# Layer 1's first norm ahead of the biases, and score matmuls with 64 keys, in a kernel of two layers on Trainium2

## The chip, the cores and the metric

The kernel runs on one core of one Trainium2 chip, as one launch. The metric is the time of a run on the device in microseconds (us). Times before are those of three runs; beside them stands one execution that the hardware profiler recorded.

## What is computed

The input x is an image of 64 by 64 places with 256 channels, all in float32. Two layers follow one another. The places are called tokens in layer 1 (4096 tokens of 256 channels).

```
# layer 0: group norm, then a linear attention over boxes of the image
q, k = sigmoid(Wq xn), sigmoid(Wk xn);  v = Wv xn / |v|        # 8 heads of 32 channels
for w in (1, 2, 4):                # box of 64/w by 64/w places around each place, edge padded
    out_w = q . boxsum(k v^T) / (q . boxsum(k) + 1e-6)
x = x + Wout concat(out_1, out_2, out_4) + bout
# layer 1: attention, then a mixture of experts
t = t + softmax(q k^T / 16) v W_out + b_out,   (q, k, v) = norm(t) w_qkv + b_qkv
t = t + sum over the best 2 of 8 experts:  weight * (gelu(xe W1 + b1) W2 + b2),  xe from norm(t)
```

In layer 0 the kernel doesn't form the box sums for every place alone: it multiplies queries with single keys, masks the scores by what lies in the box, and multiplies with v, for the parts of a box that whole-cell sums don't cover. So both layers have scores, keys times queries.

## The kernel before

The engines are called PE (matmuls), PEld (its weight loads), DVE (vector), ACT (scalar), POOL and SP. The image is cut into 8 chunks of 512 tokens, each of 4 tiles of 128 tokens; a tile is two cells of 64 tokens. The 8 heads are worked in two halves (g) of four heads; a head's 32 channels lie on 32 partitions, so four heads fill the 128 partitions. A scheduler that orders the instructions stands between this text and the engines: each engine has one queue, worked in order, and the order in it follows from the program's order and from what each instruction waits for. `tc.issue_after(ins)` puts what follows behind `ins` in its engine's queue, without a wait of its own.

**Layer 0.** `prepare` (L307) makes sigmoid(q), sigmoid(k) and v for one half: `by_channel` (L353) computes q and k and its activation at L365 is the sigmoid. `attend` (L584) makes scores, masks them and multiplies with v, for boxes of three reaches. A step holds one or more pieces (up to 512 queries together). For the edges in y (L612) the scores of a tile are made 64 keys at a time: a matmul loads 32 partitions by 64 columns of k as weights and streams the queries. For the edges in x (L681) they are made 128 keys at a time. `masked` (L548) multiplies with the masks: DVE from PSUM directly, or ACT copies (L557) and POOL multiplies (L561). The products with v are at L643 and L697. Divisions (L721, L728) and projections (L734, L738) of a strip are chores between later steps. A root of one number at L252 lets ACT load the table of the square root early in layer 0, where L158 needs it.

**The seam.** When layer 0's last projection has freed its memory, the weights and biases of layer 1 are requested (L792 to L816, on the queues of ACT and SP). Then come, in the text's order: the biases of q and k turned to columns (L818, L820), products of the router's weights with ones and with the output bias (L827), the output weights turned (L841, L842) and multiplied with the router's (L846, L853). Then the norm: `begin(c)` takes the statistics of a chunk's four tiles (L764, L765), adds 1e-5 (L769) and takes the root on ACT (L770). The loop over chunks calls `begin` one chunk ahead, takes the reciprocal (L773), norms each tile (L869), turns it (`to_channels`, L779, ACT's copy L780), makes q and k for the chunk (L885, DVE adds the bias at L889 and takes the peak at L890), then v and the router's raw logits (L896, L903, L904).

**The attention of layer 1.** Loops: 8 chunks of queries (qc), 2 halves (g), 32 tiles of keys (i); one i is called a turn here, one (qc, g) a block. A turn makes the scores of four heads for 128 keys and 512 queries (L994), two heads to each pair of PSUM banks, of which there are three. ACT takes the Exp of each pair (L1004) into one of four buffers `pe`. DVE adds `pe` to a running total (L1011, all tiles but the first and last of a block). The products with v of the turn before (L962) follow the scores on PE. Denominators are made at the end of a block, and during the blocks with g = 1 the projection of an earlier chunk is slipped in four times (L943).

A float32 matmul appears in the trace as two records, one for each pass, each with its own weight load. The experts (L1428 to L1465) and the output (L1505 to L1512) follow; the change doesn't touch them.

Of the kernel before, what the change touches and what calls it, by code (L numbers as in the profile page):

```python
# [22 lines left out]
F32 = mybir.dt.float32  # L23
# [7 lines left out]
P = 128  # L31
# [83 lines left out]
def tile_conv_attn_hybrid(ctx: ExitStack, tc: tile.TileContext, a: dict, out: bass.AP):  # L115
# [73 lines left out]
    with ExitStack() as phase:  # L189
# [23 lines left out]
        with (  # L213
# [34 lines left out]
                )  # L248


            root = small.tile([P, 1], F32, name="root")
            nc.scalar.sqrt(root, ident[:, :1])  # L252


# [43 lines left out]
        def residual(b):  # L298

            for i in range(NCH):  # L300
                last = nc.vector.transpose(
                    t[:, NB * i + b, :C].rearrange("p (j c) -> p j c", c=D),
                    rows[:, b].rearrange("p j (y i c) -> p j y i c", y=4, c=SW)[:, :, :, i, :],
                )
            return last.ins

        def prepare(g, prep, ps):  # L307

# [44 lines left out]
            def by_channel(n, i):  # L353

                pr = two_banks()
                for j in range(2):
                    for k in range(KC):
                        nc.tensor.matmul(
                            pr[:, j, :],
                            w3[:, k, n, :],  # L360
                            act[:, k, chunk(i + j)],
                            start=k == 0,
                            stop=k == KC - 1,
                        )
                nc.scalar.activation(qk[:, n, CH * i : CH * (i + 2)], pr.rearrange("p j n -> p (j n)"), AF.Sigmoid)  # L365


            st = prep.tile([P, NCH, SW, D], F32, tag="st", name="st", bufs=2)
# [215 lines left out]
        def attend(g, work, ps, qk, v, ssum, rec, woT):  # L584
# [6 lines left out]
            for w in (2, 1, 0):  # L591
# [71 lines left out]
                for ix in range(NCH):  # L663
# [12 lines left out]
                    for step in steps:  # L676
                        scs = [score() for _ in range(4)]
                        at, places = 0, []
                        for n, i, c0, c1, *mk in step:
                            for h in range(4):  # L680
                                nc.tensor.matmul(  # L681
                                    scs[h][:, at : at + n],
                                    kT[hs[h], tok(i)],
                                    qT[hs[h], CH * ix + CELL * c0 : CH * ix + CELL * c1],
                                    start=True,
                                    stop=True,
                                    skip_group_check=True,
                                )
                            places.append((at, n, i, c0, c1, *mk))
                            at += n  # L690
                        sms = masked(work, scs, at, joined((p[0], p[1], *p[-2:]) for p in places))
                        step_done()

                        def use(places=places, sms=sms, acc=acc, begun=begun, ix=ix, last=step is steps[-1], raw=raw, r=r):
                            for at, n, i, c0, c1, *_ in places:
                                for h in range(4):
                                    nc.tensor.matmul(  # L697
                                        acc[hs[h], CELL * c0 : CELL * c1],
                                        v[:, i, hs[h]],
                                        sms[h][:, at : at + n],  # L700
                                        start=not begun[0],
                                        stop=last and at == places[-1][0],
                                        skip_group_check=True,
                                    )
                                begun[0] = True
                            if last and r > 1:
                                nc.vector.tensor_add(raw[:, ix, :], acc, raw[:, ix, :])
                            elif last:
                                nc.scalar.copy(raw[:, ix, :], acc)

                        behind(lambda: None, use)
# [35 lines left out]
        for g in range(KC):  # L747
            with tc.tile_pool(name="c_prep", bufs=1) as prep, psum("c_ps1", 2) as ps:
                of = prepare(g, prep, ps)
            with tc.tile_pool(name="c_work", bufs=1) as work, psum("c_ps2", 1) as ps:  # L750
                attend(g, work, ps, *of)

# [22 lines left out]
    def to_channels(src, dst, ps):  # L775

        tp = ps.tile([P, CH], F32, tag="mm", name="ps_mm")
        for k in range(KC):
            nc.tensor.transpose(tp[:, tok(k)], src[:, tok(k)], ident)  # L779
        nc.scalar.copy(dst, tp[:, :C].rearrange("p (k n) -> p k n", k=KC))  # L780

    norm2 = Norm(keep, "ln2")


    with ExitStack() as phase:
# [15 lines left out]
        with (  # L801
# [12 lines left out]
            bo = row_on_all("L1_attn_b_out", C, win)  # L814
            bv = win.tile([P, C], F32, name="bv")
            nc.scalar.dma_start(bv, a["L1_attn_b_qkv"][2 * C :].partition_broadcast(P))  # L816
            tp = ps.tile([P, CH], F32, tag="mm", name="ps_mm")
            nc.tensor.transpose(tp[:, :6], rows6, ident[:6, :6])  # L818
            bqk = win.tile([P, 6], F32, name="bqk")
            nc.vector.tensor_copy(bqk, tp[:, :6])  # L820

            rp = ps.tile([P, CH], F32, tag="mm", name="ps_mm")
            for n, by in enumerate((lambda k: ones[:, :1], lambda k: bqk[:, 4 + k : 5 + k])):
                for k in range(KC):
                    nc.tensor.matmul(  # L827
                        rp[:, NE * n : NE * (n + 1)],
                        by(k).to_broadcast([P, P]),
                        wr[:, k, :],  # L830
                        start=k == 0,
                        stop=k == KC - 1,
                    )
            nc.vector.tensor_copy(wr_sum, rp[:, :NE])
            bo_wr = win.tile([P, NE], F32, name="bo_wr")
            nc.vector.tensor_copy(bo_wr, rp[:, NE : 2 * NE])
            woT = win.tile([P, KC, C], F32, name="woT")
            for j in range(KC):
                tp = ps.tile([P, CH], F32, tag="mm", name="ps_mm")
                for k in range(KC):  # L840
                    nc.tensor.transpose(tp[:, tok(k)], wo[:, k, tok(j)], ident)  # L841
                nc.vector.tensor_copy(woT[:, j, :], tp[:, :C])  # L842
            tp = ps.tile([P, CH], F32, tag="mm", name="ps_mm")
            for k in range(KC):
                for j in range(KC):
                    nc.tensor.matmul(  # L846
                        tp[:, NE * k : NE * (k + 1)],
                        woT[:, j, tok(k)],
                        wr[:, j, :],
                        start=j == 0,  # L850
                        stop=j == KC - 1,
                    )
            nc.vector.tensor_copy(wo[:, :, C:], tp[:, : KC * NE].rearrange("p (k e) -> p k e", e=NE))  # L853

            norm = Norm(small, "ln1")

# [4 lines left out]

            begin(0)
            for c in range(NCH):
                if c + 1 < NCH:
                    begin(c + 1)
                norm.end(NB * c, NB * (c + 1))
                for i in range(NB * c, NB * (c + 1)):
                    hn = work.tile([P, C], F32, name="hn")
                    nc.vector.tensor_scalar(  # L869
                        hn,  # L870
                        t[:, i, :C],
                        norm.mean[:, i : i + 1],
                        norm.rstd[:, i : i + 1],
                        op0=ALU.subtract,
                        op1=ALU.mult,
                    )
                    to_channels(hn, act[:, :, tok(i)], ps)

                    nc.gpsimd.tensor_add(t[:, i, :C], t[:, i, :C], bo)
                for s in range(2):  # L880
                    for g in range(KC):
                        m = KC * s + g
# [10 lines left out]
                for i in range(NB * c, NB * (c + 1)):  # L893
                    pv = ps.tile([P, CH], F32, tag="mm", name="ps_mm")
                    for k in range(KC):
                        nc.tensor.matmul(  # L896
                            pv[:, : C + NE],
                            act[:, k, tok(i)],
                            wqkv[:, k, 2 * C :],
                            start=k == 0,  # L900
                            stop=k == KC - 1,
                        )
                    nc.vector.tensor_add(v[:, i, :], pv[:, :C], bv)  # L903
                    nc.scalar.copy(t[:, i, C:], pv[:, C : C + NE])  # L904


            on_experts = lambda z: z.unsqueeze(2).to_broadcast([P, NT, NE])
# [41 lines left out]
        with tc.If(tame > 0) as branch:  # L949
            with (  # L950
# [33 lines left out]
                for qc in range(NCH):  # L984
                    for g in range(KC):
# [4 lines left out]
                        for i in range(NT):  # L990
                            sc = [two_banks() for _ in range(2)]
                            for hd in range(4):
                                hs = slice(D * hd, D * (hd + 1))
                                nc.tensor.matmul(  # L994
                                    sc[hd // 2][:, hd % 2, :],
                                    qk[hs, 1, g, tok(i)],
                                    qk[hs, 0, g, chunk(qc)],
                                    start=True,
                                    stop=True,
                                )  # L1000
                            pe = work.tile([P, 4, CH], F32, name="pe", bufs=4)
                            pairs = [slice(0, 2), slice(2, 4)]
                            for pair, s in zip(pairs, sc):
# [543 lines left out]
```

## Time and profile before

| what | us |
|---|---|
| median of three runs | 2913.63 |
| lowest and highest of them | 2911.81, 2914.61 |
| the profiled execution's own time | 2911.62 |
| its span in the profile | 2909.8 |
| PE busy in the span | 2769.2 |
| DVE busy | 2082.3 |
| ACT busy | 1529.6 |
| POOL busy | 712.4 |

The span runs from the first to the last instruction that the profile shows; the profiled execution's own time is 1.8 us longer than it. Times in views of the profile count from the start of the span. In a timeline a row is: start, length of the merged group, engine, line, operation, what it writes and reads, how many instructions, and in brackets the idle time before it and what ended that. Matmuls overlap in the array and their ends are modelled, so the starts of two groups tell more than a group's length. In a table by stage each engine's busy time stands with its number of instructions, then the granted clock of PE (1.00 is full), the share of the DMA engines and GB/s.

### The profile page before, as it was taken

What the parts mean: (1) busy time and instruction counts of PE and PEld (TensorE: products, weight loads), DVE (VectorE), ACT (ScalarE), POOL (GpSimd) and SP (SyncE); (2) the same over time, 40 slices, a digit from 0 to 9 for tenths busy, and PEclk for the clock granted to TensorE, in tenths of its full rate; (3) what the DMA queues carried; (4) which work ended last, traced back from release to release, by engine and by line L of the source; (5) the groups of instructions that cost most, each with busy time, mean ns of one, the idle gap of its engine ahead of it and who ended that gap; (6) DMA issues with size and microseconds to landing.
All of it is one profiled execution on the core that took longest, in us unless ns stands there. A gap on an engine that the chain in (4) does not pass through costs nothing. (4 is left out here: it accounts for less than half of the span.)

```text
span 2909.8 us, 62928 instructions
## 1 busy us (share of the span) xinstructions
PE 2769.2 (95%) x26286; PEld 1329.9 (46%) x26286; DVE 2082.3 (72%) x3009; ACT 1529.6 (53%) x2134; POOL 712.4 (24%) x808
## 2 busy tenths in 40 slices
PE   6899999989999988999999999999999969999996
PEld 5466442735644254222222222222222248888884
DVE  6776777577676886999999999999999941111113
ACT  3242323124233312888888888888888642222222
POOL 1085858109485711000000000000000012222220
PEclk9999999999999999999999999999999969999997
DMA  5000000000000000000000000000000056565665
GB/s 143 6 2 3 2 3 2 7 0 3 4 2 3 1 19 1 1 5 6 5 5 5 5 5 5 5 5 5 5 5 5 10 176 215 190 203 196 205 213 189
DMA packets 97546, 136.31 MB, mean 47 GB/s; under 512 B 18115, under 2 KB 79145, under 8 KB 97253
## 3 DMA queue, kind: packets, MB, share of 16 engines
q1 hardware_dynamic: 82360, 105.34, 11.2%
q0 software_dynamic: 6528, 17.83, 2.2%
q10 hardware_dynamic: 8364, 9.02, 0.9%
q8 instruction: 209, 3.42, 0.5%
q14 instruction: 85, 0.69, 0.1%
HBM read 114.57 MB, written 17.60 MB: 45 GB/s over the span
## 5 line engine op out<-in xcount | busy, mean ns | idle before, releaser
L1004 ACT ACTIVATE pe<-ps_two 128x1024 f32<-128x1024 f32 x1024 | 993.1, 1022 | 152.2 <-PE ps_two L994 146.9
L1011 DVE TENSOR_TENSOR total<-total,pe 128x1024 f32<-128x1024 f32 x928 | 1058.2, 1219 | 2.2 <-ACT pe L1004 2.2
L994 PE MATMUL ps_two<-qk 32*128 32x512 f32 x4096 | 630.6, 640 | 3.5 <-POOLq L949 1.8
L962 PE MATMUL ps_acc<-pe,v 128*32 128x512 f32 x4096 | 547.2, 605 | 0.1
L557 ACT COPY sm<-ps_sc 128x384 f32<-128x384 f32 (+4 forms) x486 | 232.5, 513 | 460.6 <-PE ps_sc L681 271.2
L561 POOL TENSOR_TENSOR sm<-sm,mask 128x192 f32<-128x192 f32 (+3 forms) x460 | 380.2, 860 | 232.7 <-ACT sm L557 232.5
L994 PEld LDWEIGHTS ps_two<-qk 32*128 32x128 f32 x4096 | 205.2, 183 | 419.5 <-PE ps_two L994 221.3
L561 DVE TENSOR_TENSOR sm<-ps_sc,mask 128x384 f32<-128x384 f32 (+3 forms) x708 | 324.1, 518 | 92.8 <-PE ps_sc L681 91.4
L1456 ACT ACTIVATE hid<-ps_hp,cols 128x256 f32<-128x256 f32 (+1 forms) x288 | 133.1, 462 | 360.4 <-PE ps_hp L1453 359.3
L1271 POOL MEMSET on<- 128x256 f32 x1 | 0.3, 311 | 1177.3 <-PE ps_den L962 1177.3
L962 PEld LDWEIGHTS ps_acc<-pe,v 128*32 128x32 f32 x4096 | 80.8, 108 | 390.3 <-issue 377.2
L681 PE MATMUL ps_sc<-qk 32*128 32x192 f32 (+3 forms) x2688 | 245.3, 446 | 5.7 <-DVE sm L561 2.9
L1453 PE MATMUL ps_hp<-xe,w 128*128 128x256 f32 (+1 forms) x1152 | 246.6, 370 | 0.0
L1462 PE MATMUL ps_yp<-w,hid 128*128 128x256 f32 x1088 | 240.8, 379 | 0.0
L1453 PEld LDWEIGHTS ps_hp<-xe,w 128*128 128x128 f32 x1152 | 201.1, 190 | 39.7 <-ACT hid L1456 5.6
L697 PE MATMUL ps_acc<-sm,v 128*32 128x192 f32 (+3 forms) x2688 | 216.6, 423 | 0.8 <-POOL sm L561 0.8
L1462 PEld LDWEIGHTS ps_yp<-w,hid 128*128 128x128 f32 x1088 | 204.2, 190 | 26.4
L1432 DVE TENSOR_SCALAR xe<-ps_tp,cols 128x256 f32<-128x256 f32 (+1 forms) x72 | 34.8, 525 | 239.3 <-PE ps_tp L1428 217.5
L561 POOL TENSOR_TENSOR sm<-sm,ycut 128x384 f32<-128x384 f32 (+4 forms) x150 | 150.8, 1024 | 140.9 <-ACT sm L557 140.6
L681 PEld LDWEIGHTS ps_sc<-qk 32*128 32x128 f32 x2688 | 126.3, 186 | 124.5 <-DVE sm L561 70.1
L561 DVE TENSOR_TENSOR sm<-ps_sc,ycut 128x512 f32<-128x512 f32 (+4 forms) x250 | 127.7, 562 | 65.2 <-PE ps_sc L612 63.2
L1464 DVE TENSOR_TENSOR y<-ps_yp,b 128x256 f32<-128x256 f32 x68 | 28.9, 425 | 195.1 <-PE ps_yp L1462 195.1
(239 smaller groups left out, 2244.3 us busy)
## 6 DMA issues: line engine op xcount, KB each, us to landing
w<-in_L_ffn_W SPq DMA_DIRECT2D x72, 1024.0 KB
b<-in_L_ffn_b SPq DMA_DIRECT2D x36, 128.0 KB
rows<-in_x SPq DMA_DIRECT2D x16, 256.0 KB
zrows<-act SPq DMA_DIRECT2D x4, 1024.0 KB
y<-yrows SPq DMA_DIRECT2D x8, 512.0 KB
y<-yrows ACTq DMA_DIRECT2D x8, 512.0 KB
rec<-recs SPq DMA_DIRECT2D x60, 64.0 KB
x<-in_x ACTq DMA_DIRECT2D x4, 512.0 KB
```

The source lines that it names most:

```text
L557: nc.scalar.copy(sm[:, :used], sc[:, :used])
L561: engine.tensor_mul(to, of, mk.unsqueeze(1).to_broadcast(list(to.shape)))
L681: nc.tensor.matmul(scs[h][:, at : at + n], kT[hs[h], tok(i)], qT[hs[h], CH * ix + CELL * c0 : CH * ix + CELL * c1], start=True, stop=True, ...
L697: nc.tensor.matmul(acc[hs[h], CELL * c0 : CELL * c1], v[:, i, hs[h]], sms[h][:, at : at + n], start=not begun[0], stop=last and at == plac ...
L962: nc.tensor.matmul(to[D * hd : D * (hd + 1), :], lhsT(hd), rhs[:, hd, :], start=start, stop=stop, skip_group_check=True,)
L994: nc.tensor.matmul(sc[hd // 2][:, hd % 2, :], qk[hs, 1, g, tok(i)], qk[hs, 0, g, chunk(qc)], start=True, stop=True,)
L1004: nc.scalar.activation(pe[:, pair, :], s, AF.Exp, scale=C**-0.5)
L1011: add = nc.vector.tensor_add(to, first[:, pair, :] if i == 1 else to, pe[:, pair, :])
L1432: nc.vector.tensor_scalar(xe[:, k, :n], tp[:, k, :n], cols[:, gain], cols[:, shift], op0=ALU.mult, op1=ALU.add,)
L1453: nc.tensor.matmul(hp[:, :n], w1[:, k, tok(m)], x_now[:, k, :n], start=k == 0, stop=k == KC - 1)
L1456: nc.scalar.activation(hid[:, m, :n], hp[:, :n], AF.Gelu, bias=cols[:, m : m + 1])
L1462: nc.tensor.matmul(yp, hid[:, m, tok(j)], w2[:, m, :], start=m == 0, stop=m == NH - 1)
```

## The change

Four things are changed.

- In `attend` the scores of a step with a single piece are made 64 keys at a time (two matmuls with half the weights each); other steps keep 128.
- In the attention of layer 1 all scores are made 64 keys at a time.
- The root of one number is taken a second time, behind the last sigmoid of the second half of layer 0.
- At the seam the text's order is changed: statistics, norm and turning of chunk 0 come first, with four buffers for normed tiles; the bias columns and the statistics of chunk 1 are put behind them, and the router's products behind chunk 0's v.

```
-            root = small.tile([P, 1], F32, name="root")
+            root = wts.tile([P, 1], F32, name="root")
             nc.scalar.sqrt(root, ident[:, :1])
...
+        sigmoid = [None]
...
-                nc.scalar.activation(qk[:, n, CH * i : CH * (i + 2)], pr.rearrange("p j n -> p (j n)"), AF.Sigmoid)
+                sigmoid[0] = nc.scalar.activation(qk[:, n, CH * i : CH * (i + 2)], pr.rearrange("p j n -> p (j n)"), AF.Sigmoid).ins
...
                         for n, i, c0, c1, *mk in step:
+                            rows = CELL if len(step) == 1 else P
                             for h in range(4):
-                                nc.tensor.matmul(
-                                    scs[h][:, at : at + n],
-                                    kT[hs[h], tok(i)],
-                                    qT[hs[h], CH * ix + CELL * c0 : CH * ix + CELL * c1],
...
+                                for u in range(0, P, rows):
+                                    nc.tensor.matmul(
+                                        scs[h][u : u + rows, at : at + n],
+                                        kT[hs[h], P * i + u : P * i + u + rows],
+                                        qT[hs[h], CH * ix + CELL * c0 : CH * ix + CELL * c1],
...
                 of = prepare(g, prep, ps)
+            if g == KC - 1:
+                with tc.issue_after(sigmoid[0]):
+                    nc.scalar.sqrt(root, ident[:, :1])
...
+            def biases():
+                tp = ps.tile([P, CH], F32, tag="mm", name="ps_mm")
+                nc.tensor.transpose(tp[:, :6], rows6, ident[:6, :6])
+                nc.vector.tensor_copy(bqk, tp[:, :6])
+
+            def router():
...
             begin(0)
             for c in range(NCH):
-                if c + 1 < NCH:
+                if 0 < c < NCH - 1:
                     begin(c + 1)
                 norm.end(NB * c, NB * (c + 1))
                 for i in range(NB * c, NB * (c + 1)):
-                    hn = work.tile([P, C], F32, name="hn")
-                    nc.vector.tensor_scalar(
+                    hn = work.tile([P, C], F32, name="hn", bufs=4)
+                    last = nc.vector.tensor_scalar(
...
-                    to_channels(hn, act[:, :, tok(i)], ps)
+                    turned = to_channels(hn, act[:, :, tok(i)], ps)
...
+                if c == 0:
+                    with tc.issue_after(last.ins), tc.issue_after(turned.ins):
+                        biases()
+                        begin(1)
...
+                if c == 0:
+                    with tc.issue_after(biased.ins), tc.issue_after(product.ins):
+                        router()
...
                             for hd in range(4):
                                 hs = slice(D * hd, D * (hd + 1))
-                                nc.tensor.matmul(
-                                    sc[hd // 2][:, hd % 2, :],
-                                    qk[hs, 1, g, tok(i)],
-                                    qk[hs, 0, g, chunk(qc)],
...
+                                for u in range(2):
+                                    nc.tensor.matmul(
+                                        sc[hd // 2][CELL * u : CELL * (u + 1), hd % 2, :],
+                                        qk[hs, 1, g, P * i + CELL * u : P * i + CELL * (u + 1)],
+                                        qk[hs, 0, g, chunk(qc)],
```

The body of `router` is what stood before the norm: the products of L827, the turning of L841 and L842, the products of L846 and their copies. `turned` is the last matmul of a tile's turning; `product` and `biased` are the last matmul and the last addition of v in the chunk.

## Prediction

> **What bounds the kernel now.** I read the page first (busy shares and clock by slice), then busy time by stage, then the timeline of two places: one turn of the long loop of layer 1, and the seam between the layers. The chain of waits on the page ends in the last 48 us, which the change doesn't touch, so it is of no use here.
>
> By stage (length, then PE, PE's loads, DVE, ACT, POOL, granted clock, DMA):
>
> ```profile
> 1030.00:1043.00 13.00, 7.00 (x30) 5.84 (x31) 8.93 (x42) 3.29 (x8) 2.90 (x4) 0.61 0.33 103
> 1043.00:1147.00 104.00, 95.52 (x314) 54.94 (x314) 80.57 (x185) 15.11 (x66) 20.91 (x28) 0.98 0.00 1
> 1147.00:2316.00 1169.00, 1166.78 (x8564) 314.05 (x8565) 1128.82 (x1075) 1010.63 (x1056) 0.78 (x4) 1.00 0.02 5
> ```
>
> The attention of layer 1 (third row) is 40% of the span. PE is never idle in it, but DVE is busy for 1128.8 of 1169 us too: whatever PE gives up there, DVE caps. The timeline of one turn (one tile of 128 keys for four heads):
>
> ```profile
> 1499.61 1.94 ACT L1004 ACTIVATE pe<-ps_two 128x1024 f32<-128x1024 f32 x2 [0.21 <-PE ps_two L994]
> 1500.59 0.39 PEld L994 LDWEIGHTS ps_two<-qk 32*128 32x128 f32 x8 [0.84 <-issue]
> 1500.60 1.22 PE L994 MATMUL ps_two<-qk 32*128 32x512 f32 x8
> 1501.74 0.16 PEld L962 LDWEIGHTS ps_acc<-pe,v 128*32 128x32 f32 x8 [0.76 <-issue]
> 1501.74 1.06 PE L962 MATMUL ps_acc<-pe,v 128*32 128x512 f32 x8
> 1501.77 1.94 ACT L1004 ACTIVATE pe<-ps_two 128x1024 f32<-128x1024 f32 x2 [0.22 <-PE ps_two L994]
> ```
>
> Scores start at 1500.60, products with v at 1501.74, the next scores at 1502.74: a turn of 2.15 us. The eight score matmuls are four heads in two passes each. Layer 0 shows the same scores with 128 and with 64 keys:
>
> ```profile
> 425.89 0.90 PE L612 MATMUL ps_sc<-qk 32*64 32x384 f32 x16
> 426.72 0.98 PE L643 MATMUL ps_acc<-sm,v 64*32 64x448 f32 x16
> ...
> 994.86 0.93 PE L681 MATMUL ps_sc<-qk 32*128 32x384 f32 x8
> 995.72 1.06 PE L697 MATMUL ps_acc<-sm,v 128*32 128x512 f32 x8
> 996.71 1.14 PE L681 MATMUL ps_sc<-qk 32*128 32x512 f32 x8
> 997.78 0.85 PE L697 MATMUL ps_acc<-sm,v 128*32 128x384 f32 x8
> ```
>
> Read starts, since ends are modelled: 384 queries take 0.83 us with 64 keys (425.89 to 426.72) and 0.86 with 128; 512 with 128 take 1.07. And the seam:
>
> ```profile
> 1031.70 1.28 ACT L770 ACT_TABLE_LOAD   x1 [23.84 <-DVE ln_mv L765]
> 1033.00 0.20 ACT L770 ACTIVATE ln_rstd<-ln_rstd 128x4 f32<-128x4 f32 x1
> 1035.27 0.24 PE L818 MATMUL ps_mm<-cst,bias_rows 6*128 6x6 f32 x1 [5.90 <-DMA bias_rows<-in_L_attn_b_out]
> 1035.62 0.17 DVE L820 COPY bqk<-ps_mm 128x6 f32<-128x6 f32 x1 [2.18 <-PE ps_mm L818]
> 1037.51 0.40 DVE L869 TENSOR_SCALAR hn<-t,ln_mv,ln_rstd 128x256 f32<-128x256 f32 x1
> 1042.79 9.01 PE L885 MATMUL ps_mm<-act,wqkv 128*128 128x512 f32 x16 [0.46 <-ACT act L780]
> ```
>
> The first root is done at 1033.2, but DVE stands in the copy of the biases until a DMA lands; the first norm starts at 1037.51, the first q/k product at 1042.79.
>
> **The skill.** "TensorE: Matmul & The Clock Gate", section "LDWEIGHTS (loading the stationary operand)": a load's time goes with the columns loaded, columns / 1.2 ns, not with the rows. The trace agrees in the slope: 184, 131 and 109 ns for 128, 64 and 32 columns. "TensorEngine Tiling (Array Packing)", "Key Properties": tiles load and multiply in parallel, and a change of tiling mode drains the engine. Both are seen: the eight tiles of an L612 pass start 7 ns apart, and a group after another mode starts about 90 ns after its predecessor's streaming, alike for 64 and 128 columns. The change adds no such switch. "TensorE: Matmul & The Clock Gate", "Part 1: The HAM clock gate (the "warmup" mystery)": idle windows of 3413 ns, free-running, halve the clock, and a busy one restores it. Agrees: half clock from 1032.9 to 1046.6, four windows. "ScalarE: Activation LUTs", "What ACT_TABLE_LOAD costs": 1283 ns and a drain; the trace has 1.28 us and no drain visible at this place.
>
> **64 keys in layer 1.** 2048 score matmuls become 4096 (512 turns, 8 for 4). The single records give the cost. With 128 columns a pass of 512 queries takes 533 ns to the next pass of the same heads: 427 of streaming and 106 of exposed load. With 64 columns a pass of 384 takes 376 (eight starts over 49 ns, then 327): 320 and 56. So 50 ns less per pass, and the last of twice as many tiles starts later (7 ns each).
>
> What of it shortens a turn? Heads 2 and 3 start 90 ns after heads 0 and 1 (1500.687 against 1500.596): they need the bank pair that the first Exp of the previous tile is reading. This is a loop over two turns: heads 0/1 to their Exp 1.174 (1500.596 to 1501.770); Exp to heads 2/3 of the next tile 1.077 (1499.611 to 1500.687); heads 2/3 to the products 1.058 (to 1501.745); products to the next heads 0/1 0.996. Sum 4.305, 2.152 a turn, against alternating turns of 2.145 and 2.185 measured: this loop sets the pace. The first and third term each hold one exposed load: each loses 50 and gains 14 (two more starts), 36 ns. Per turn (36+36)/2 = 36 ns; 512 turns 18.4 us. 60 turns, with a denominator (32: 256 records, eight each) or a projection in them (28: 112 records of L943, four each), have no such wait and save only what layer 0 shows, 27 ns: 18.4 - 60 x 0.009 = 17.9.
>
> DVE's cap: in each block of 32 tiles its adds (1.14 us, two a tile) fall behind the Exp. In the block from 1437.45 the add of tile 28 ends 1.28 us before the Exp that reuses its buffer. Over the 31 turns up to there 0.036 x 31 = 1.1 us of that goes; 0.15 is left, about a semaphore's time. I take off 0.4 for it: **-17.5**. Bounds: -13 (only 27 ns a turn and some loss to DVE) and -22 (block cap 1.28 and a little, times 16).
>
> **64 keys in layer 0.** Only steps with one piece: 80 with 384 queries (0.858 to 0.831, -27 ns) and 32 with 512 (1.071; 64 columns estimated from 0.831 and 0.937 at 384 and 448 as 1.044, -27). 112 x 0.027 = **-3.0** where PE is continuous, as it nearly is; the mixed steps keep 128. Bounds 0 and -4: the masks on POOL are the next to be late (1.1 us each, 1.5 a step of 1.85).
>
> **Root table.** The load and root go behind the last sigmoid of the second half of layer 0. ACT is idle there from 626.8 to 643.2, which hides 1.5 us whole; without that cover the first mask copy would be that late. It stays loaded, as only copies follow. At the seam a load of 1.28 goes.
>
> **First chunk ahead.** The built order (the change fixes orders on one engine; no wait is added): DVE has four tiles' statistics, add, reciprocal, four norms; PE has eight transposes, the bias transpose, then the q/k products; chunk 1's statistics and the bias copy follow on DVE. Statistics end at 1031.85, root about 1032.15, first norm 1032.4; four at 0.36 end at 1033.9 (four buffers, no wait). Eight transposes at half clock (0.27) run from 1032.8 to 1035.0, the last copy ends about 1035.6. The bias transpose is queued ahead of the products, and its rows land at 1035.24 as before (no DMA is moved): 1035.5. The weights' last packet is at 1033.8, visible about 1.2 later as with the biases. First product 1035.9, 6.9 earlier. Paid back: 20 small router records (8, 4, 8) now stand between chunk 0's products and chunk 1's. They took 0.23 each at half clock, so some 0.12 at full, 2.5 us with the wait for the two copies of the turned weights, part of it covered by chunk 1's transposes (bounds 1.5 and 4.5). Half clock lasted 3.8 us into the products; it can now last 3.4 to 6.8, 5.1 on average: half of 1.3, +0.7. **-3.7**, bounds -0.5 and -6. POOL's residual adds follow the norms and aren't late.
>
> **Sum.** -17.5 - 3.0 - 3.7 = -24.2. The profiled execution took 2911.62 (span 2909.8 and 1.8 around it), 2.0 under the median of 2913.63. After: 2887.4 by the profile, **2889.4** as median.
>
> **Rivals.** (a) Attention saves half or less, since ACT or DVE takes the place of the wait: DVE's 97% speaks for it, 1.28 us of slack against. -8 for attention, -15 in all: 2899. (b) More: the half-clock windows at the seam and at 1149 to 1155.8 (3.4 us lost) fall away, and the slack is used up to -21: 2880. (c) Slower: the two halves of a head share a row group and, in a loop of 1100 us instead of short steps, their loads don't overlap. Of a load 78 ns stay hidden now (184 - 106), so a pass would expose 2 x 131 - 78 = 184 ns: +78 in each of the two terms, and +14 for the starts, halved +92 a turn. 512 turns make +47, less 6.7 elsewhere: 2954. It decides from 92 ns exposed on (106 - 14), where a turn gains nothing. Against it: L612's eight loads of a pass expose 56. (d) Nothing: L612 wins by its small steps only and the seam's gain goes to the router; 2911.
>
> **Chances.** Forecast 0.64 (2882 to 2896), (a) 0.16, (b) 0.10, (c) 0.06, (d) 0.04. Range 2879 to 2902: it leaves out (c), (d) and the ends of (a) and (b). About 0.2% (5.8 us) is what a measurement can tell from no change: faster 0.90, same 0.04, slower 0.06.
>
> **What would show it.** Right: turns of 2.11 to 2.12 and the stage from 1169 to about 1151; score records 32*64 with passes 483 ns apart; 112 layer-0 steps 27 ns shorter; no table load at the first norm, first q/k product 6 to 7 us after the last projection instead of 13.4, router records behind chunk 0. Wrong: ACT waits ended by DVE (the cap bites), turns of 2.15 or more, or passes over 533 ns apart.

## The result and the profile after

The changed kernel takes **2897.26 us** (median of 6 runs, 2895.58 to 2899.96) where the kernel before takes 2912.81 (6 runs, 2910.74 to 2914.61). The ratio is 0.9947, 95% interval [0.9934, 0.996]. The forecast of 24.2 us less had the right sign and, in the main, the right mechanism; 15.6 us came. The execution that was profiled took 2897.41 us with a span of 2895.6 (before: 2911.62 and 2909.8).

Cut at the same events in both traces (starts of PE's records), the span divides like this:

| stage, us | before | after | difference | forecast |
|---|---|---|---|---|
| start to last projection of layer 0 | 1029.0 | 1030.6 | +1.6 | -3.0 |
| to the first q/k product of layer 1 | 13.80 | 7.41 | -6.4 | -6.9 |
| to the first score of layer 1 | 104.46 | 104.04 | -0.4 | +3.2 |
| first to last score of layer 1 | 1161.09 | 1154.16 | -6.9 | -17.5 |
| to the end | 601.5 | 599.5 | -2.0 | 0 |

The first row varies for the same code (two kernels below that leave layer 0 as it was have 1025.4 and 1033.0 there), so it needs more than one trace; it gets them below. The last row varies too (599.4 to 602.2 in e1, e2, e3, e9, e10 and e12, all with the same code there), so its 2.0 can't be read as a gain.

The stages of the kernel after, as those of before were shown (length, then PE, PE's loads, DVE, ACT, POOL, granted clock, DMA):

```profile
1030.00:1038.00 8.00, 3.08 (x15) 2.26 (x13) 6.39 (x22) 1.69 (x5) 0.12 (x1) 0.73 0.55 166
1038.00:1142.00 104.00, 98.31 (x335) 57.76 (x335) 85.67 (x205) 14.56 (x67) 23.60 (x32) 0.97 0.00 1
1142.00:2303.00 1161.00, 1159.14 (x12654) 275.26 (x12656) 1128.02 (x1074) 1009.52 (x1056) 0.48 (x3) 1.00 0.02 6
```

The seam went from 13 to 8 us. The second stage kept its 104 us although PE has 21 more records in it: it was idle for 8.5 us of them before and is for 5.7 now. In the third, DVE's busy time is what it was (1128), and the stage is 8 us shorter, so DVE's share rose.

PE's timeline of some turns of layer 1:

```profile
1528.07 1.11 PE L1017 MATMUL ps_two<-qk 32*64 32x512 f32 x16
1529.12 1.06 PE L983 MATMUL ps_acc<-pe,v 128*32 128x512 f32 x8
1530.11 1.31 PE L1017 MATMUL ps_two<-qk 32*64 32x512 f32 x16
1531.35 1.06 PE L983 MATMUL ps_acc<-pe,v 128*32 128x512 f32 x8
```

Take the starts again. The scores of one turn need 1.04 to 1.05 us (1528.07 to 1529.12), as layer 0 had promised; those of the next need 1.24 (1530.11 to 1531.35), because heads 2 and 3 wait for an Exp. Single records show second passes 480 ns behind the first where 533 were before (forecast 483). Yet the mean turn is 2.143 us, not 2.11 to 2.12. So PE's part came as forecast and the wait for Exp got longer.

Layer 0 after the change:

```profile
994.78 0.90 PE L686 MATMUL ps_sc<-qk 32*64 32x384 f32 x16
995.62 1.06 PE L702 MATMUL ps_acc<-sm,v 128*32 128x512 f32 x8
```

This step of 384 queries takes 0.84 us. Over all of them the median falls from 0.858 us to 0.831 (80 steps of 384) and from 1.089 to 1.052 (32 of 512): the forecast's 27 ns a step are there, and a little more in the longer steps. And the seam:

```profile
1033.65 0.20 ACT L779 ACTIVATE ln_rstd<-ln_rstd 128x4 f32<-128x4 f32 x1 [24.25 <-DVE ln_rstd L778]
1034.17 1.38 DVE L882 TENSOR_SCALAR hn<-t,ln_mv,ln_rstd 128x256 f32<-128x256 f32 x4
1037.80 0.24 PE L833 MATMUL ps_mm<-cst,bias_rows 6*128 6x6 f32 x1 [1.13 <-DMA bias_rows<-in_L_attn_b_qkv]
1037.97 3.78 PE L903 MATMUL ps_mm<-act,wqkv 128*128 128x512 f32 x4
```

No table load stands ahead of the root; the four norms follow it at once; PE is held back by the biases' rows and then starts the products. The router's products come from 1051.42 on, behind chunk 0.

### The profile page after: what moved, and what is told of

Same layout as the page of the kernel before. It is cut to its first block, busy times and chain, and to the rows that moved or that the text cites. A ratio compares the mean times of both kernels' runs of the same rounds, so it can differ in the third digit from the quotient of the medians.

```text
span 2895.6 us, 73117 instructions
## 1 busy us (share of the span) xinstructions
PE 2757.3 (95%) x31278; PEld 1282.3 (44%) x31278; DVE 2083.0 (72%) x3009; ACT 1527.4 (53%) x2135; POOL 711.5 (25%) x808
## 3 DMA queue, kind: packets, MB, share of 16 engines
q1 hardware_dynamic: 82360, 105.34, 11.4%
## 5 line engine op out<-in xcount | busy, mean ns | idle before, releaser
L1017 PE MATMUL ps_two<-qk 32*64 32x512 f32 x8192 | 623.3, 614 | 2.8 <-POOLq L970 1.9
L1017 PEld LDWEIGHTS ps_two<-qk 32*64 32x64 f32 x8192 | 166.1, 130 | 423.5 <-PE ps_two L1017 377.3
L686 PE MATMUL ps_sc<-qk 32*64 32x384 f32 (+3 forms) x3584 | 241.2, 461 | 4.6 <-DVE sm L563 2.9
L563 DVE TENSOR_TENSOR sm<-ps_sc,ycut 128x512 f32<-128x512 f32 (+4 forms) x250 | 127.9, 562 | 70.9 <-PE ps_sc L614 69.3
L686 PEld LDWEIGHTS ps_sc<-qk 32*64 32x64 f32 (+1 forms) x3584 | 116.9, 159 | 123.2 <-DVE sm L563 70.1
```

The lines of the kernel that those rows point to most:

```text
L563: engine.tensor_mul(to, of, mk.unsqueeze(1).to_broadcast(list(to.shape)))
L686: nc.tensor.matmul(scs[h][u : u + rows, at : at + n], kT[hs[h], P * i + u : P * i + u + rows], qT[hs[h], CH * ix + CELL * c0 : CH * ix + C ...
L1017: nc.tensor.matmul(sc[hd // 2][CELL * u : CELL * (u + 1), hd % 2, :], qk[hs, 1, g, P * i + CELL * u : P * i + CELL * (u + 1)], qk[hs, 0, g ...
```

## The experiments

The kernel before was run beside each of these on the same chip. Its own time differs from one group of runs to the next (2909.7 to 2912.8), so gains are given against the runs beside them.

| kernel | median, us | against before | ratio, 95% |
|---|---|---|---|
| after | 2897.26 | -15.6 | 0.9947 [0.9934, 0.9960] |
| e1: 64 keys in layer 1 alone | 2899.75 | -11.4 | 0.9960 [0.9946, 0.9973] |
| e2: 64 keys in layer 0 alone | 2912.06 | +0.9 | 1.0000 [0.9992, 1.0009] |
| e3: seam and root alone | 2902.90 | -8.3 | 0.9969 [0.9957, 0.9981] |
| e4: after, one increment for each pair | 2894.98 | -16.2 | 0.9942 [0.9928, 0.9955] |
| e5: after, no fallback branch | 2886.80 | -22.9 | 0.9925 [0.9911, 0.9938] |
| e6: e5 with fewer additions | 2881.29 | -28.5 | 0.9902 [0.9887, 0.9918] |
| e7: before, no fallback branch | 2905.86 | -3.9 | 0.9986 [0.9978, 0.9995] |
| e8: e4 with additions on POOL | 2942.30 | +32.6 | 1.0121 [1.0105, 1.0136] |
| e9: after, 64 keys later in layer 0 | 2890.86 | -20.9 | 0.9937 [0.9923, 0.9951] |
| e10: seam alone, no root in layer 0 | 2905.50 | -6.2 | 0.9978 [0.9971, 0.9986] |
| e11: fallback ahead of the attention | 2894.04 | -17.7 | 0.9945 [0.9931, 0.9959] |
| e12: after, layer 0 with 128 keys | 2894.47 | -16.2 | 0.9947 [0.9933, 0.9960] |

**The three parts alone (e1, e2, e3).** Each takes one part of the diff onto the kernel before and leaves the rest of it as it was.

> The change's 64 keys in layer 1's attention alone. In the profile of the changed kernel the stretch from the first to the last score of this stage went from 1161.1 to 1154.2 us, so if the parts add up: 6.9 us faster than before (2906), and the same stretch in the profile (1154). If the forecast's 36 ns a turn were there and were only hidden by another part of the change: 17 us faster (2896).

> The change's 64 keys in layer 0 alone. Forecast: 112 steps x 27 ns = 3.0 us faster (2910). Rival: the profile of the changed kernel has layer 0's last projection 1.6 us later than before, so the steps do not decide and the time is the same or up to 2 us longer. If the half-clock windows of the profiled execution made that delay (48 us of them in layer 0 in place of 37, half of the difference is 5 us), this profile's layer 0 goes with its own half-clock windows, and the steps with 384 queries take 0.831 us.

> The order at the seam and the root table alone, 128 keys everywhere. The profile of the changed kernel has 111.5 us from the last projection of layer 0 to the first score of the attention, 118.3 before: 6.8 us faster if the parts add up (2906). The forecast had 3.7 (2909): then the router's products are paid back in full behind chunk 0.

Attention gives 11.4, the seam 8.3, layer 0 nothing that can be measured. The seam is twice the forecast, attention two thirds of it. e1 lies between its two expectations, e3 gains more than both of its own, and e2 is its rival's case. The parts sum to 18.8, a little over the 15.6 of the whole, within the intervals. Part of the excess is the clock: the runs of e1 and e3 were granted 0.9738 and 0.9737 of full clock in the mean, the runs of before beside them 0.9730 and those of after 0.9728. That is some 4 to 5 us less at half clock, an estimated 1 to 1.5 us each (the last section has the price).

**Why attention fell short: increments (e4, e5, e7).** In the trace of after, the first Exp follows the last matmul of its pair at four distances: 0.654 us (100 turns), 0.680 (206), 0.706 (77) and 0.732 (125). In two turns of a block (tiles 3 and 5) it comes 60 ns later still, in the kernels before and after alike and for no cause that was found. The built program explains the steps. An Exp waits for a semaphore that PE's matmuls raise. Of the four second-pass matmuls of a pair, sometimes only the last one raises it (once for all four), sometimes two, three or all four raise it by one each; the four distances belong to one, two, three and four such increments. Before, a pair had two matmuls: 0.634 with one increment (263 turns), 0.660 with two (247). So an increment of its own costs **26 ns**, and two more tiles of half the width 20. Why not always one? The likely reason is the Else (the fallback for large scores, not taken here): it shares the semaphore's counts with the If, so that counts in between are kept. e4 and e5 show that the separate increments go when the Else goes; the reason itself is argued. The Trainium skill, "TensorE: Matmul & The Clock Gate", section "The cost: per-tile semaphore tail", has this very cost: increments of tiles serialize, at an estimated 26.3 ns each, and the tiles themselves 4.7. The trace agrees on the first; two more tiles took 20 ns here. The prediction didn't use it.

e4 keeps all of the computation, but puts the fallback under a condition of its own:

```
-        with tc.If(tame > 0) as branch:
+        with tc.If(tame > 0):
...
-        with branch.Else():
+        with tc.If(tame < 1):
```

> The changed kernel, with the fallback attention in an If of its own behind the first in place of the Else; all of the computation is kept. In the built program the score matmuls of a head pair then raise PE's semaphore once, at the last of them; in the changed kernel they do it one to four times. Theory 1: each separate increment holds the Exp back by 26 ns (Exp comes 0.654, 0.680, 0.706, 0.732 us after the last second-pass matmul of its pair for 1, 2, 3, 4 increments in the profile of the changed kernel). On average Exp starts 1.192 us after the first score, with one increment 1.154: half of 38 ns a turn, 9.6 us less than the changed kernel, 25 less than before (2888). Theory 2: the Exp is late because eight tiles share the array's way out, and increments are only counted alongside: no difference from the changed kernel (2897).

All turns show 0.654 (tiles 3 and 5 again 60 ns more), and the mean turn falls from 2.143 to 2.123 us, 36 ns under the 2.159 of before (inner turns of blocks without projections, from Exp to Exp, the first block left out). The Exp of the turn of after that starts at 1528.07 above, with two increments, and below it a turn of e5, with one:

```profile
1529.25 1.94 ACT L1028 ACTIVATE pe<-ps_two 128x1024 f32<-128x1024 f32 x2 [1.35 <-PE ps_two L1017]
...
1527.94 1.11 PE L1017 MATMUL ps_two<-qk 32*64 32x512 f32 x16
1529.10 1.94 ACT L1028 ACTIVATE pe<-ps_two 128x1024 f32<-128x1024 f32 x2 [0.27 <-PE ps_two L1017]
```

From the first score to the Exp it is 1.18 us in the first and 1.16 (1.154 in single records) in the second. But the time fell by only 0.6 more than in after, where 9.6 had been expected. Part went where the condition stands: last score to the hidden products took 70.9 us where it had been 66.1. The rest went to the ends of the blocks, below. e5 leaves the fallback branch out altogether (that part is not computed), and e7 does the same to the kernel before:

```
-        with branch.Else():
-            ...
```

> The kernel after with the fallback branch (attention for scores too large for the plain exponential) left out, so that part is not computed and the score matmuls need only one increment for each pair. Theory 1 (separate increments cost 26 ns each; the run with a second condition in place of Else lost 4.5 us at that condition): turns of 2.123 us and block ends of 17.0 us as with the second condition, the attention about 4.0 us shorter than in the kernel after, and last score to the first record of the hidden products back at 66.1 instead of 70.9; in all 2889 to 2891. Rival (the 4.5 us belong to the faster attention, for instance DVE's backlog at its end, and not to the condition): 2894 to 2896.

> The kernel before with the fallback branch left out, so that part is not computed: one increment for each pair instead of one or two. Theory 1 (26 ns for each separate increment ahead of the Exp): before, about half the pairs wait for two, so the first term of the loop loses 13 ns, turns go from 2.159 to 2.150, the attention loses 3 to 5 us, in all about 2908. Then 64 keys with single increments are worth 27 ns a turn and not 36. Rival (the increments only matter with 64 keys): 2911 to 2913.

e5 has the turns of e4 and 65.2 us behind the last score, and is at -22.9 where e4 is at -16.2: that stage of the trace puts the condition at 5.7 us, the runs of the two differ by 6.7. e7's turns fall from 2.159 to 2.154 (2.150 was expected) and its attention from 1161.09 to 1158.01, as expected: the increments cost the kernel before 3 to 4 us as well. With single increments on both sides (e7 to e5), 64 keys are worth 30.5 ns a turn: first scores to Exp 1.174 to 1.154 (-20), heads 2/3 to products 1.058 to 1.017 (-41), and half of the sum of 61. The prediction's loop is right there to the nanosecond or two: its terms sum to 4.305, and half of that, 2.152, is the turn of e7.

**DVE at the block ends (e6, e8).** Divide each block into inner turns (tiles 3 to 27) and the seven others. Those seven took 16.78 us before, 16.77 after, 16.99 in e4 and e5 in the mean of the blocks without projections, though each of their turns has less work on PE. (After, most blocks have 16.68, and two have 0.3 more.) The waits of three kernels, from 1160 to 2290 us (us in total, times, longest), before:

```profile
PEld ps_den L943 <- DVE total L1011: 10.1, 12, 0.8
DVE total L1011 <- PE ps_den L962: 7.4, 4, 1.9
```

after:

```profile
PEld ps_den L964 <- DVE total L1035: 17.6, 21, 0.8
DVE total L1035 <- PE ps_den L983: 1.2, 1, 1.2
```

and e5:

```profile
PEld ps_den L964 <- DVE total L1035: 17.6, 21, 0.8
DVE total L1035 <- PE ps_den L983: 17.0, 14, 1.2
ACT rec L1074 <- PE ps_den L983: 5.3, 14, 0.5
```

In e5 DVE finishes a block's sums late, PE's denominators and ACT's copy of them wait for it, and DVE can't start the next block's sums before PE has read the old ones: 14 times, 1.2 us each. A pair of blocks loses 0.97 us from e7 to e5 (145.20 to 144.23), where 64 turns at 30.5 ns would be 1.95: half of the gain goes at the block ends. e6 takes work from DVE alone. It leaves the additions of three tiles out of the denominators of each block:

```
-                            elif i < NT - 1:
+                            elif i < NT - 1 and i not in (8, 16, 24):
```

> The kernel without the fallback branch, and the additions of three of the 30 tiles of each block left out of the denominators (tiles 8, 16, 24): DVE has 6.8 us less in a block, PE and ACT the same work. Theory 1 (with 64 keys and single increments, DVE's backlog takes back about 0.5 to 1.1 us at each of the 16 block ends): inner turns unchanged at 2.12, block ends from 17.0 to 16.0 to 16.5, in all 8 to 16 us less than the kernel without the fallback branch. Rival (block ends are PE's own work, DVE's wait is hidden): within 2 us of it.

The block ends fall from 16.99 to 16.5, the inner turns rise from 2.123 to 2.130, and a pair of blocks from 144.23 to 143.54: eight pairs make 5.5 us, and the runs give the same (2886.80 to 2881.29, beside the same runs of before). The wait of DVE for PE is gone from e6's list. So DVE's cap is real in e5, but smaller than the 8 to 16 us that were expected, and inner turns got longer by 7 ns, which was not. That it also took from the kernel after is argued from the waits above (PE's for the sums, 10.1 us before and 17.6 after). e8 tries to use this with all of the computation kept: POOL makes three of the 60 additions of a block.

```
+                                helped = (8, 16, 24)
+                                for pair in pairs[:: -1 if i - 1 in helped else 1]:
...
+                                    by = nc.gpsimd if i in helped and pair.start == 0 else nc.vector
```

> All of the computation kept: the second condition in place of Else, and of tiles 8, 16 and 24 of each block the addition of heads 0 and 1 is made by POOL, which is idle there, with DVE's next two additions exchanged so that it doesn't wait. DVE has 3.4 us less in a block. Theory 1 (DVE's backlog at block ends): turns 2.12, block ends 16.2 to 16.7 instead of 17.0, in all 5 to 12 us less than with the second condition alone (2895), so 2883 to 2890. Rival (POOL's additions slow DVE's by sharing memory ports, or DVE waits for POOL): 2893 to 2905.

It took 33 us more than before, far outside both of its ranges. The durations in e8 (shortest, median, longest in ns, then first and last start):

```profile
L1036 DVE TENSOR_TENSOR total<-total,pe x880: 1157/1212/3215, 1146.7 to 2341.4; 128x1024 f32<-128x1024 f32 x176
...
L1036 POOL TENSOR_TENSOR total<-total,pe x48: 3112/3220/3228, 1159.5 to 2323.7; 128x1024 f32<-128x1024 f32 x48
```

POOL needs 3.2 us for an addition, and the DVE addition that runs beside one takes 3.2 instead of 1.2. One of each pair of engines waits for the other to finish: the slow DVE addition starts 1.1 us into POOL's and ends 1.08 us after it. 48 such additions cost DVE 48 x 2.0 = 96 us and save it 48 x 1.2 = 58: a loss of 38, and the attention is 46 longer than in e4. The Trainium skill, "SBUF — State Buffer", section "Who interferes with whom", says as much: a DVE instruction with two inputs in SBUF contends with a GpSimd instruction that reads SBUF, and the one that comes second blocks. It should have settled the expectation.

**The seam (e10).** e10 is e3 without the root in layer 0.

> The seam's new order alone, without the root in layer 0, so the load of the root's table is back ahead of the first norm; both attentions with 128 keys. Theory 1: the load of 1.28 us stands on the path of the first norm, so the first q/k product comes 1.3 us later than with the root (6.6 to 7.4 after the last projection become 8 to 8.6), in all 1.0 to 1.5 us more than the seam with the root. Rival (statistics or the biases' transfer set the first product): no change, within 0.5 us.

e10's seam:

```profile
1035.68 1.28 ACT L772 ACT_TABLE_LOAD   x1 [23.83 <-DVE ln_mv L767]
1035.85 0.17 DVE L771 TENSOR_SCALAR ln_rstd<-ln_mv 128x4 f32<-128x4 f32 x1
1036.97 0.21 ACT L772 ACTIVATE ln_rstd<-ln_rstd 128x4 f32<-128x4 f32 x1
1037.49 1.38 DVE L875 TENSOR_SCALAR hn<-t,ln_mv,ln_rstd 128x256 f32<-128x256 f32 x4
```

The load begins ahead of the root's input, which is written from 1035.85 for 0.17 us, and holds the root until 1036.97: some 0.9 of its 1.28 us are exposed. Counted from the last projection, the first norm starts 0.9 us later than in e3 (4.53 against 3.62). At the first product less of it is left: e10 has 7.50, the nine kernels with the root 6.56 to 7.41, 6.98 in the mean. In seven of these nine PE's last wait ahead of the products is for the biases' rows, as in after above, so the rival is partly right. Up to the first score e10 needs 110.7 us; the eight kernels with the root (without e11, whose condition stands there) need 110.3 in the mean (109.6 to 111.5), and the four with the old order 118.5. So in these traces the root's place is worth about half a microsecond, less than their scatter, and the order of the chunks nearly all of the seam's 8.2. The runs of e3 and e10 differ by 2.1, with intervals that overlap.

**Layer 0 (e9, e12).** In all six profiles with 64 keys in all 112 steps of layer 0, the last run of y steps of the first half takes 77.1 to 78.3 us; in the other eight profiles it takes 74.5. That code was not changed. The extra time lies in three places, of which this is one, after:

```profile
421.60 0.66 PE L645 MATMUL ps_acc<-sm,v 64*32 64x256 f32 x15
423.26 0.40 PE L645 MATMUL ps_acc<-sm,v 64*32 64x256 f32 x1 [1.00 <-issue]
423.59 0.63 PE L614 MATMUL ps_sc<-qk 32*64 32x448 f32 x8
```

and before:

```profile
421.88 0.66 PE L643 MATMUL ps_acc<-sm,v 64*32 64x256 f32 x16
422.47 1.01 PE L612 MATMUL ps_sc<-qk 32*64 32x448 f32 x16
```

The sixteenth matmul of a group comes 1.4 us behind the fifteenth, and PE waits for nothing that the profile shows ("issue"). Most such stalls of this stage stand in or just behind bursts of 128 small matmuls (L633 here, L631 before) in every kernel, before too, but at other places.

e9 takes the 40 steps of 384 queries of the first half back to 128 keys, e12 takes back all 112:

```
-                            rows = CELL if len(step) == 1 else P
+                            rows = CELL if len(step) == 1 and (g == KC - 1 or step[0][0] == CH) else P
```

```
-                            rows = CELL if len(step) == 1 else P
+                            rows = P
```

> The kernel after, with layer 0's steps of 384 queries in its first half back at 128 keys (40 steps; the 72 others keep 64). Theory 1 (the 64 keys' own gain is there, but the longer instruction stream shifts three stalls of PE, in which it waits for nothing the profile shows, into the third run of y steps of the first half, 78.0 us instead of 74.5): that run is back at 74.5, the x run ahead of it grows from 65.3 to about 66.2, layer 0 gains 2 to 3 us, in all 2894 to 2895 when after is 2897. Rival (the y run is longer because of what follows or precedes it on other engines, or by chance): y run 77 to 78, in all within 1 us of after plus 1.

> The kernel after with all of layer 0's scores back at 128 keys: the seam, the root and 64 keys in the attention of layer 1 stay. Theory 1 (the parts add up: seam 8.3 and attention 11.4 by their own runs, and layer 0's part gives its 3 us back in stalls of PE): third y run of the first half 74.5, about 2892 by the sum of the parts, so 64 keys in layer 0 cost after a few us net, and restricting them to the steps behind that run (2890.9) is worth 1 to 3 more. Rival (layer 0's part is worth its 3 us here too): 2899 to 2901.

In both the y run is back at 74.5. From the first score to the last one of the first half, and from there to the last projection in the second, the attention of layer 0 takes (means over executions, granted half clock 10 to 17 us in each):

| layer 0's scores | kernels | first half, us | second half | sum |
|---|---|---|---|---|
| 128 keys | before, e1, e3, e7, e10, e12 | 362.3 | 386.1 | 748.4 |
| 64 keys in 112 steps | after, e2, e4, e5, e6, e8 | 363.1 | 383.7 | 746.8 |
| 64 keys behind the y run | e9, e11 | 361.8 | 383.7 | 745.5 |

The second half gains 2.4. The first half loses 0.8: its last y run is 3.1 us longer in the mean, so its other runs gain 2.3. Net -1.6 of the forecast -3.0, while single executions of one row differ by 3 to 5 us in the sum, and neither pair of runs shows a gain: e2 is at +0.9, and e12's runs can't be told from after's (-16.2 against -15.6). So e12 failed as a test of size: neither of its expectations was met by the runs, and only its trace speaks. e9's restriction gives 1.3 more by this table; its runs say 5.3 more than after, where 2 to 3 had been expected. Part of the rest is the clock: e9's runs were granted 0.9742 in the mean and after's 0.9728, about 8 us less at half clock, an estimated 2 to 3 us. Whether the edit or chance gave that is open. What PE waits for in a stall, an instruction that isn't there yet or something else, stays open; no run took the stalls away by themselves.

**A better place for the condition (e11).** e11 puts the fallback, with a condition of its own, ahead of the attention, with layer 0 as in e9.

```
+        with tc.If(tame < 1):
+            ...
         with tc.If(tame > 0):
...
-        with branch.Else():
-            ...
```

> All of the computation kept: the fallback branch stands under a condition of its own AHEAD of the attention instead of as its Else, so that each pair needs one increment, and the cost of the second condition falls next to a wait for the same value; layer 0 as in the kernel with 128 keys in its first half's steps of 384. Theory 1: attention as without the fallback (turns 2.123, 1147 to 1150), last score to hidden products 65 to 66, first q/k product to first score 1 to 4 us longer than 104; layer 0 gains 2 to 3 us; in all 2886 to 2890, better than after (2897) and than the second condition behind (2895). Rival (each condition costs some 5 us wherever it stands): 2890 to 2893.

Last score to hidden products is 64.2, but first product to first score rose from 103.2 in e9 to 108.2: the condition costs its 5 us there instead (a part of it through half clock, 13.0 us of the seam against 6.8). The rival's mechanism holds, though the total (2894.04) lies above its numbers too. Of the kernels with the whole computation e9 has the lowest time, 2890.86 us, below both before and after; e5 and e6 are faster, but leave part of the computation out.

## Why the prediction was right in kind and wrong in size

**64 keys in layer 1: -17.5, measured about -8 to -11.** The loop over two turns was the right model, and its third term fell by 41 ns (forecast 36). The failed step is "the first and third term each hold one exposed load: each loses 50 and gains 14". For the first term, heads 0/1 to their Exp, it took the distance from the last matmul to the Exp as fixed. That distance grew by 20 ns for the tiles and by 26 for each further increment, and the term went from 1.187 to 1.192 us in the mean, +5 and not -36. Half of (+5 - 41) is 18 ns, against 16 measured (2.159 to 2.143). e4 and e5 show it from the other side: with one increment the turn loses the 36 ns. The prediction took its first term, 1.174, from one turn with a single increment; the mean of before was 1.187, since 247 turns had two. The two turns that it set beside its sum (2.145 and 2.185) are from a stretch with 2.119 to 2.186; the mean of before is 2.159. A pair of blocks lost 1.00 us (145.59 to 144.59); eight pairs are 8.0. The attention stage shows 6.9, with 3.4 us more at half clock, worth about 1.1 (see the end).

**DVE's cap: 0.4 allowed, more measured, in e5.** The 0.4 assumed that the cap acts where an Exp needs a buffer. It acts at the end of a block, where denominators wait for the sums. Seven turns at the end of a block should have lost 7 x 27 ns = 0.19 us and lost 0.10 in most blocks, in the mean 0.01 in those without projections and 0.09 in the others: some 1.4 to 2.2 us short over 16 blocks. That DVE is the cause in after was not tested. In e5, with faster turns, e6 prices the cap at 5.5.

**Layer 0: -3.0, measured -1.6 in the mean of traces and nothing in the runs.** The step "112 single-piece steps times 27 ns" held in the steps; "where PE is continuous" did not: 3.5 us of the trace of after (3.1 in the mean of six) went to stalls of PE in code that the change doesn't touch. What was named as the next to be late, POOL's masks, was not it.

**Seam: -3.7, measured -6.8 in the trace of after, -8.2 in the mean of traces and -8.3 in the runs of e3.** The way to the first product came out as forecast: root at 1033.65 without a load, first product 6.4 us earlier against 6.9 (7.1 in the mean of traces), though it was the biases' rows that came last there, about 1 us later than before and than forecast (7.24 us after the last projection against 6.28), and not the turned norms. The failed term is the router's, +2.5: its products did go behind chunk 0, but into idle time of PE, which the row of 104 us with 95.5 of PE had shown. First product to first score went from 104.5 to 103.3 us in the mean of traces, where 3.2 more had been forecast. Also the half clock's +0.7 didn't show as a longer stage, though half clock lasted 5.9 us into the products (forecast 5.1 on average).

**Root's table: 0 in layer 0.** Right: no stage of layer 0 shows it, and e10 gives its worth at the seam: 0.9 of the 1.28 us at the first norm, about half a microsecond in the mean at the first product.

**Rivals.** (a) was the nearest: half of attention's gain lost, since another engine takes the place of the wait, 2899. Its cause was wrong in the kernel after, where the increments took most, and right in e5. (b) to (d) are out: passes are 480 ns apart, so loads overlap, and the seam's gain stayed. That the total came within the stated 2879 to 2902, if outside the forecast's own 2882 to 2896, is in part luck: attention and layer 0 gave some 8 to 13 us less than forecast, and the seam 3 to 5 more.

## What to carry to other kernels

When an edit splits a matmul into more tiles, price two things apart: what PE issues, and how long after the last tile the reader may start; count which matmuls raise the semaphore in the built program, since here separate increments stood on single tiles only as long as an Else that is never taken was there. Ahead of adding work behind a seam, look at PE's idle time in the stage that receives it, and before giving an idle engine a share, look for what it shares with the loaded one. When the bounding wait shrinks, ask at which point of the loop the nearly full engine must be done, not only whether its average fits.

## What the runs showed of the hardware that had not been expected

- A separate semaphore increment by a matmul delays the waiting Exp by 26 ns: 0.634 and 0.660 us before; 0.654, 0.680, 0.706 and 0.732 after.
- A second condition with an untaken body costs about 5 us: behind the attention 70.9 us in e4, 66.1 in after and 65.2 in e5; ahead of it 108.2 in e11 and 103.2 in e9, where e11 also had 6 us more at half clock.
- At half clock the attention loses about a third of the time, up to 0.45 of it: 1159.0 us with none of it (e3 and e10) and 1161.1 with 6.8 us of it (before), 1151.4 with 3.4 (e9) and 1154.1 with 10.2 (after and e12), 1147.0 with none (e5) and 1150.1 with 6.8 (e4), the same code of the attention in each pair.
- DVE and POOL additions with both inputs in SBUF run one after the other: 1.2 us becomes 3.2 beside POOL's 3.2.
- PE stalls of about 1 to 1.7 us without a shown cause stand mostly in or just behind bursts of 128 matmuls of 64 columns, at places that move when other code grows.
